# Attention and a routed mixture of experts on one core: small slot tiles in column groups, w2 loaded by turns, another start

## The chip, the cores and the metric

The kernel runs on one core of one Trainium2 chip. The metric is the device time of an execution in microseconds, lower being better. Three runs of the kernel before took 748.45, 749.07 and 749.04 us; the median is 749.04.

## What is computed

The reference, cut to what matters (B = 16 batches of S = 128 tokens, D = 256):

```python
# attention, 16 heads of 64: the latents are the normed x, the context is ctx
x_n = layer_norm(ctx, ln1_w, ln1_b)
lat = layer_norm(layernorm(x), ln2_w, ln2_b) * (1 + cond) + cond
q   = lat @ Wq.T
k, v = split(concat(x_n, lat) @ Wkv.T)
x   = x + softmax(q @ k.T / 8) @ v @ Wo.T
# experts: 8 routed, of which each token takes one, and a shared one; F = 704
h      = layernorm(x)
scores = h @ router                       # best expert, gate = sigmoid(best score)
routed = (silu(g*h @ w1[e]) * (g*h @ w3[e])) @ w2[e]
shared = (silu(h @ ws1) * (h @ ws3)) @ ws2
out    = x + shared + routed
```

All data are float32.

## The kernel before, in words

The order of the instructions on every engine is written out by hand. [...]

**Start.** `idle_ps` (L99 to L100) is a row of WARM = 9 matmuls on zeros. The first two batches' x and ctx and the constants `vec`, and the weights wk, wv, wq, wo, come over the SP and ScalarE queues (L281 to L294). `first_inputs(i)` (L387) makes the normed, transposed and modulated inputs `kvT` of batch i: statistics on VectorE (DVE), a reciprocal root by `newton` (L121, twelve DVE steps on 128x2 values), scaling (`normed`, L139), transposes on TensorE into a PSUM tile `fkvt` (L410), and modulation (L416 on DVE, L418 on ScalarE). Then come the projections `k_unit` (L440), `v_unit`, `q_unit`.

**Attention.** `step` (L788) handles half the heads of a batch: logits, maxima, exponents, normalising, turning through DRAM, and the weighted sum `weigh` (L556). Projections of the next batches, output projections (`finish`) and units of the shared expert are put between as `units`. `weigh` writes two heads into rows 0 to 63 and 64 to 127 of one PSUM tile, two matmuls of 64 columns.

PSUM has three pools: `ps_m` (three buffers, one bank each) for most products, `ps_s` (two buffers of two banks) for logits and the experts' up-projections, and `ps_o`.

**Routing.** `route` (L997) runs on DVE beside units of the shared expert. It finds each token's expert, sorts the experts by load into windows 0 to 7, and gives each token a slot. Window w has WINDOWS[w] slots: 320, 288, 288, 288 and four times 256. Slots are held in tiles: tiles 2w and 2w+1 have 128 rows; the rest of windows 0 to 3 (64, 32, 32, 32 rows, `REST`) lies in tiles 16 to 19, one for each window. So there are 20 tiles, four of them small. `slot_table` (L954) builds a table of token numbers and gates by 16 matmuls `slots` (L983) from `at_row` (L976).

**Experts.** `load_experts` (L920) loads w2 of all eight experts into `wds` ahead of the routing; `load_up` loads w1 and w3 of a window's expert into one of three buffers, at an address that SP reads from the routing. The rows of h are gathered by GpSimd (`gather`, L1188), multiplied by their gates and transposed: for window 0 on TensorE (`transpose_inputs`, L1207, tile `px`), for the others by DVE and a way through DRAM (`turn_inputs`, `fetch_inputs`). In the loop over windows (L1319), `up` (L1243) makes the hidden values `mid_w` in six parts f; after part 0 of window w come the down-projections of window w-1 (`down_window`, `out_rows` L1276): six matmuls `yr` for each tile (L1279), whose stationary operand is the tile's hidden values, 128, 64 or 32 columns wide, and whose moving operand is w2, 256 wide. Its address in `wds` comes from a register of TensorE's sequencer, read at L1320. DVE adds the gathered shared part, and GpSimd scatters the rows to the output. There are two buffers each of inputs and hidden values. `ending` closes with the last block of the shared expert.

The lines for the small tiles:

```python
def tiles_of(w):
    return [2 * w, 2 * w + 1] + ([2 * E + w] if REST[w] else [])
def rows_of(t):
    return P if t < 2 * E else REST[t - 2 * E]
```

Of the kernel before, what the change touches and what calls it, by code (L numbers as in the profile page):

```python
# [20 lines left out]
WARM = 9  # L21
# [6 lines left out]
def resampler_attn__then__top1_moe_kernel(  # L28
# [40 lines left out]
    NTILE = 2 * E + NREST  # L69
# [189 lines left out]
    with ExitStack() as at:  # L259
# [17 lines left out]
        wk = wts.tile([P, DC, INNER], F32, name="wk")  # L277
# [5 lines left out]
        nc.scalar.dma_start(out=vec, in_=vecs)  # L283
        nc.sync.dma_start(out=wk, in_=wkv_t[:, 0:INNER].rearrange("(c p) e -> p c e", p=P))
        nc.scalar.dma_start(out=tokens[0][:, 1, :], in_=lat_ctx[1])
        nc.sync.dma_start(out=xres[0][:, 1, :], in_=x[1])
        nc.scalar.dma_start(
            out=wv, in_=wkv_t[:, INNER : 2 * INNER].rearrange("(c p) e -> p c e", p=P)
        )
        nc.scalar.dma_start(out=wq, in_=wq_t.rearrange("(c p) e -> p c e", p=P))  # L290
        nc.sync.dma_start(out=wr, in_=router.rearrange("(c p) e -> p c e", p=P))
        nc.scalar.dma_start(out=wo, in_=wo_t.rearrange("(k p) d -> p k d", p=P))
        nc.sync.dma_start(out=h_rows[NT : NT + 1, :], in_=zero[0:1, :])
        nc.sync.dma_start(out=s_rows[NT : NT + 1, :], in_=zero[0:1, :])  # L294
# [92 lines left out]
        def first_inputs(i):  # L387
# [14 lines left out]
            for r in newton(small, v, 2, "j2"):  # L402
                pass
            z = work.tile([P, 2, D], F32, tag="z", name=f"fz_{i}", bufs=1)
            for k, t in enumerate(pair):
                normed(z[:, k, :], t, (mv[:, k, 0:1], r[:, k : k + 1]))
            for c in range(DC):
                pt = ps_m.tile([P, 2, S], F32, tag="mm", name=f"fkvt_{i}_{c}")
                for k in range(2):
                    nc.tensor.transpose(pt[:, k, :], z[:, k, ts(c, P)], ident)  # L410
                for k, (w, o) in enumerate(
                    ((vec[:, c, C_W1 : C_W1 + 1], vec[:, c, C_B1 : C_B1 + 1]),
                     (mod_w[:, c, i : i + 1], mod_b[:, c, i : i + 1]))
                ):
                    if c == 0:
                        nc.vector.tensor_scalar(kvTs[0][:, c, i, k, :], pt[:, k, :], w, o, ALU.mult, ALU.add)  # L416
                    else:
                        nc.scalar.activation(  # L418
                            kvTs[0][:, c, i, k, :], pt[:, k, :], AF.Identity, bias=o, scale=w
                        )  # L420
# [19 lines left out]
        def k_unit(b, j):  # L440
# [3 lines left out]
            for jj in range(2):  # L444
                for c in range(DC):
                    nc.tensor.matmul(  # L446
                        pk[:, jj, :],
                        lhsT=wk[:, c, ts(2 * j + jj, P)],
                        rhs=kvTs[b // 2][:, c, b % 2].rearrange("p t s -> p (t s)"),
                        start=(c == 0),  # L450
                        stop=(c == DC - 1),
                    )
# [335 lines left out]
        def step(u, units, side, loads=(), early=4, behind=(), exp_first=False):  # L788
# [15 lines left out]
            if u // 2 >= B - 2:  # L804

                nc.scalar.activation(spare[0:1, 1:2], spare[0:1, 0:1], AF.Exp)
# [38 lines left out]
        load_tokens(1)  # L845
        pieces, transpose = inputs(1)
# [6 lines left out]
        def second_inputs():  # L853
            transpose(range(DC))
            load_tokens(2)

        choose = []
        for g in range(NG):
# [9 lines left out]
            if g == 0:  # L868
                step(0, k1[:2] + [second_inputs] + k1[2:] + q[:2], [])
# [47 lines left out]
    wds = wexp.tile([P, E, NF, D], F32, name="wds")  # L917
    w13s = [wexp.tile([P, DC, 2 * F], F32, name=f"w13_{k}") for k in range(3)]

    def load_experts():  # L920
        for e in range(E):
            nc.sync.dma_start(
                out=wds[:, e, 0:FC, :],
                in_=w2[e, 0 : FC * P, :].rearrange("(c p) d -> p c d", p=P),
            )
            nc.sync.dma_start(out=wds[:, e, FC, :], in_=w2[e, F - P : F, :])
# [70 lines left out]
    def route():  # L997
# [98 lines left out]

        slot = mscratch.tile([P, B], F32, name="slot")
        nc.vector.scalar_tensor_tensor(slot, win, 2.0 * P, place, ALU.mult, ALU.add)
        shift = mscratch.tile([P, B], F32, name="shift")
        nc.vector.tensor_scalar(  # L1100
            shift, win, -float(P), float((2 * E - 2) * P), ALU.mult, ALU.add
        )
        nc.vector.scalar_tensor_tensor(shift, place, 2.0 * P, shift, ALU.is_ge, ALU.mult)
        nc.vector.tensor_tensor(slot, slot, shift, ALU.add)

        def beyond(n, w, length, name, pool):

            o = pool.tile([P, length], F32, name=name)
            for k in range(E):
                step = REST[k] - (REST[k + 1] if k + 1 < E else 0)  # L1110
                if step:
                    less = mscratch.tile([P, length], F32, tag="less", name=f"{name}{k}")
                    nc.vector.tensor_scalar(less, w, float(k + 1), float(step), ALU.is_lt, ALU.mult)
                    nc.vector.tensor_tensor(o, n, less, ALU.subtract)
                    n = o
            return o

        over = beyond(place, win, B, "over", mconst)
# [15 lines left out]
        for n, _ in enumerate(finding):  # L1134
            if n == 0:
# [15 lines left out]
                for w in range(3):  # L1151
                    load_up(w, w)
            if n == 1:

                load = beyond(total, window, E, "load", mconst)
# [9 lines left out]
        for t in tiles_of(0):  # L1165
            gather(t)
        for _ in range(4):
            yield
        for t in tiles_of(0):
            gate(t)  # L1170
        yield
        for i, t in enumerate(tiles_of(0)):
            transpose_inputs(t, inputs_t[0][:, :, ds(i * P, rows_of(t))], rows_of(t))
        for t in tiles_of(1):
            gather(t)


    xgs, ups = {}, {}
    inputs_t = [rwork.tile([P, DC, WMAX], F32, name=f"xT_{k}", bufs=1) for k in range(2)]
    x_blocks = tc.dram_tile([DC, WMAX // BL, BL, NB, BL], F32, name="x_blocks")  # L1180

    def tiles_of(w):
        return [2 * w, 2 * w + 1] + ([2 * E + w] if REST[w] else [])

    def rows_of(t):
        return P if t < 2 * E else REST[t - 2 * E]

    def gather(t, n=None):  # L1188
        n = n or rows_of(t)
        xg = rwork.tile([P, D], F32, tag="xg", name=f"xg_{t}")  # L1190
        nc.gpsimd.indirect_dma_start(
            out=xg[0:n, :],
            out_offset=None,
            in_=h_rows,
            in_offset=Offset(ap=routing["table"][0:n, t : t + 1], axis=0),
            bounds_check=NT,
            oob_is_err=False,
        )
        xgs[t] = xg

    def gate(t, n=None):
        n = n or rows_of(t)
        nc.vector.tensor_scalar(
            xgs[t][0:n, :], xgs[t][0:n, :], routing["gates"][0:n, t : t + 1], None, ALU.mult
        )

    def transpose_inputs(t, xT, n):  # L1207
        xg = xgs.pop(t)
        px = ps_m.tile([P, DC, n], F32, tag="mm", name=f"px_{t}")
        for c in range(DC):  # L1210
            nc.tensor.transpose(px[:, c, :], xg[0:n, ts(c, P)], ident[0:n, 0:n])
        nc.vector.tensor_copy(xT, px)

    def turn_inputs(w):

        for i, t in enumerate(tiles_of(w)):
            n = rows_of(t)
            gate(t)
            px = rwork.tile([P, DC, NB, BL], F32, tag="xp", name=f"xp_{t}")
            nc.vector.transpose(  # L1220
                px[0:n], xgs.pop(t)[0:n, :].rearrange("p (c k j) -> p c j k", c=DC, k=BL)
            )
            nc.sync.dma_start(
                out=x_blocks[:, ds(i * NB, n // BL)].rearrange("c i k j q -> (i k) c (j q)"),
                in_=px[0:n].rearrange("p c j q -> p c (j q)"),
            )

    def fetch_inputs(w):
        n = WINDOWS[w]
        for c in range(DC):  # L1230
            nc.sync.dma_start(
                out=inputs_t[w % 2][:, c, 0:n].rearrange("p (i q) -> p i q", q=BL),
                in_=x_blocks[c, 0 : n // BL].rearrange("i k j q -> (k j) i q"),
            )

    def load_up(k, w):
        e = nc.sync.value_load(routing["expert"][0:1, w : w + 1], min_val=0, max_val=E - 1)
# [4 lines left out]

    def up(w13, xT, n, mid, f, name):  # L1243

        ps = ps_s.tile([P, 2, 512], F32, tag="S", name=f"u_{name}_{f}")
# [18 lines left out]
    def stream_rows(t, n, table=None):  # L1264
        sg = mwork.tile([P, D], F32, tag="xr", name=f"sg_{t}", bufs=3)
        nc.gpsimd.indirect_dma_start(
            out=sg[0:n, :],
            out_offset=None,
            in_=s_rows,
            in_offset=Offset(ap=routing["table"][0:n, t : t + 1], axis=0),  # L1270
# [5 lines left out]
    def out_rows(t, n, e, mid, sg):  # L1276
        py = ps_m.tile([P, D], F32, tag="mm", name=f"yr_{t}")
        for f in range(NF):
            nc.tensor.matmul(  # L1279
                py[0:n, :],  # L1280
                lhsT=mid[:, f, 0:n],
                rhs=wds[:, ds(e, 1), f, :].rearrange("p e d -> p (e d)"),
                start=(f == 0),
                stop=(f == NF - 1),
            )
# [13 lines left out]
    load_experts()  # L1299
# [11 lines left out]
    mids = [hidden_t.tile([P, NF, WMAX], F32, name=f"mid_w{k}") for k in range(2)]  # L1311
# [3 lines left out]
    def down_window(w, sgs):  # L1315
        for i, (t, sg) in enumerate(zip(tiles_of(w), sgs)):
            out_rows(t, rows_of(t), ups[w], mids[w % 2][:, :, ds(i * P, rows_of(t))], sg)

    for w in range(E):  # L1319
        ups[w] = nc.tensor.value_load(  # L1320
# [157 lines left out]
```

## Time and profile before

| what | value |
|---|---|
| runs | 748.45, 749.07, 749.04 us |
| profiled execution, its time | 748.45 us |
| its span, first to last instruction | 746.6 us |
| granted TensorE clock, mean | 0.999 |
| first projection (pk, L446) starts | 9.32 us |
| last matmul ends | about 741.2 us |
| VectorE, ScalarE, GpSimd busy | 385.8, 259.1, 314.4 us |
| HBM read, written | 75.49 MB, 49.02 MB |

How it is read: "busy" is the time in which an engine had at least one of its instructions running; PE is TensorE's matmul stream and PEld its weight loads. A group's line gives the source line, engine, operation, out<-in, shape and the number of records, then busy time and the mean of one in ns; after a second bar stands the idle time just before. A line of the waits gives who waited for whom: us in total, times, longest. A line of the chain gives start, duration and what. Times are from the span's start. "SPq" and "ACTq" are queues that issue transfers.

### The profile page before, as it was taken

What the parts mean: (1) busy time and instruction counts of PE and PEld (TensorE: products, weight loads), DVE (VectorE), ACT (ScalarE), POOL (GpSimd) and SP (SyncE); (2) the same over time, 40 slices, a digit from 0 to 9 for tenths busy, and PEclk for the clock granted to TensorE, in tenths of its full rate; (3) what the DMA queues carried; (4) which work ended last, traced back from release to release, by engine and by line L of the source; (5) the groups of instructions that cost most, each with busy time, mean ns of one, the idle gap of its engine ahead of it and who ended that gap; (6) DMA issues with size and microseconds to landing.
All of it is one profiled execution on the core that took longest, in us unless ns stands there. A gap on an engine that the chain in (4) does not pass through costs nothing.

```text
span 746.6 us, 11560 instructions
## 1 busy us (share of the span) xinstructions
PE 736.0 (99%) x4096; PEld 572.5 (77%) x4096; DVE 385.8 (52%) x949; ACT 259.1 (35%) x787; POOL 314.4 (42%) x366
## 2 busy tenths in 40 slices
PE   8999999999999999999999999999999999999997
PEld 6857768777677677687686788688888877778886
DVE  5566558558647656665656437634643333333321
ACT  2444534444354354344444554611311011111111
POOL 1363554464355445534643654440104334444220
PEclk9999999999999999999999999999999999999999
DMA  8075735844953953864664634651991345645301
GB/s 297 17 250 195 204 128 179 235 165 154 270 170 127 264 200 129 218 223 143 193 197 137 203 124 165 208 183 56 306 322 55 83 110 154 173 138 162 97 27 46
DMA packets 140773, 125.20 MB, mean 168 GB/s; under 512 B 62484, under 2 KB 124631, under 8 KB 140708
## 3 DMA queue, kind: packets, MB, share of 16 engines
q1 hardware_dynamic: 134356, 108.49, 46.8%
q0 software_dynamic: 4336, 12.46, 5.4%
q10 hardware_dynamic: 2016, 3.43, 1.3%
q8 instruction: 35, 0.57, 0.3%
q14 instruction: 30, 0.25, 0.1%
HBM read 75.49 MB, written 49.02 MB: 167 GB/s over the span
## 4 chain that ended last, share of the span: by engine, by line
PE 93%; DVE 4%; ACT 2%; issue 0%; DMA 0%; ACTq 0%
PE pk L446 15%; PE pv L465 14%; PE u_w L1249 11%; PE S L498 8%; PE O L563 8%; PE p L162 8%; PE pw L579 7%; PE pq L431 7%; PE yr L1279 7%; PE ys L192 5%; ACT pe L517 1%; PE pr L634 1%; PE pr L162 1%; PE ys L245 1%; PE slots L983 0%
## 5 line engine op out<-in xcount | busy, mean ns | idle before, releaser
L530 POOL TENSOR_SCALAR pe<-pe,rs 128x256 f32<-128x256 f32 x256 | 232.5, 926 | 243.7 <-DVE rs L527 243.7
L517 ACT ACTIVATE pe<-S,nmx 128x256 f32<-128x256 f32 x256 | 118.7, 489 | 132.0 <-DVE nmx L510 132.0
L465 PE MATMUL pv<-wv,kvT 128*128 128x512 f32 x256 | 116.5, 599 | 0.2 <-ACT kT L454 0.2
L446 PE MATMUL pk<-kvT,wk 128*128 128x256 f32 x512 | 115.2, 383 | 1.3 <-ACT kT L454 0.7
L446 PEld LDWEIGHTS pk<-kvT,wk 128*128 128x128 f32 x512 | 95.8, 190 | 19.4 <-DVE px L539 2.0
L539 DVE STREAM_TRANSPOSE px<-pe 128x512 f32<-128x512 f32 x128 | 81.4, 682 | 32.0 <-POOL pe L530 32.0
L465 PEld LDWEIGHTS pv<-wv,kvT 128*128 128x128 f32 x256 | 47.2, 190 | 53.2 <-issue 50.6
L1249 PE MATMUL u_w<-xT,w 128*128 128x256 f32 (+2 forms) x352 | 85.6, 399 | 0.3
L1249 PEld LDWEIGHTS u_w<-xT,w 128*128 128x128 f32 x352 | 66.0, 190 | 18.8 <-DVE mid_w L1258 3.3
L510 DVE TENSOR_REDUCE nmx<-S 128x4 f32<-128x1024 f32 x64 | 75.1, 1213 | 9.7 <-PE S L498 9.5
L162 PE MATMUL p<-hT,ws 128*128 128x256 f32 x320 | 73.8, 382 | 0.2 <-DVE mid L178 0.2
L162 PEld LDWEIGHTS p<-hT,ws 128*128 128x128 f32 x320 | 59.9, 190 | 10.0 <-issue 1.3
L563 PEld LDWEIGHTS O<-pT,v 128*64 128x64 f32 x1024 | 55.2, 137 | 14.7 <-issue 12.9
L498 PE MATMUL S<-kT,qT 64*128 64x256 f32 x512 | 63.9, 389 | 0.0
L563 PE MATMUL O<-pT,v 128*64 128x128 f32 x1024 | 63.0, 276 | 0.0
L472 ACT COPY v<-pv 128x512 f32<-128x512 f32 x64 | 38.2, 599 | 63.1 <-PE pv L465 63.1
L527 DVE RECIPROCAL rs<-sums 128x4 f32<-128x4 f32 x64 | 11.4, 177 | 93.4 <-ACT pe L517 93.4
L579 PEld LDWEIGHTS pw<-wo,oT 128*128 128x128 f32 x256 | 48.6, 190 | 12.2 <-issue 3.1
L579 PE MATMUL pw<-wo,oT 128*128 128x256 f32 x256 | 57.9, 379 | 0.0
L431 PE MATMUL pq<-kvT,wq 128*128 128x256 f32 x256 | 57.7, 379 | 0.0
L1257 ACT ACTIVATE rsl_w<-u_w 128x256 f32<-128x256 f32 (+2 forms) x40 | 16.0, 400 | 118.8 <-PE u_w L1249 118.8
L517 ACT ACTIVATION_READ_ACCUMULATOR pe<-S,nmx 128x1 f32 x256 | 56.6, 221 | 0.0
(212 smaller groups left out, 748.5 us busy)
## 6 DMA issues: line engine op xcount, KB each, us to landing
p_blocks<-px SPq DMA_DIRECT2D x64, 512.0 KB, 3.2
pT<-p_blocks SPq DMA_DIRECT2D x64, 512.0 KB, 4.2
w<-in_w_dram SPq DMA_DIRECT2D x8, 704.0 KB, 6.3
wds<-in_w_dram SPq DMA_DIRECT2D x8, 640.0 KB, 8.3
w<-in_w_dram SPq DMA_DIRECT2D x8, 640.0 KB, 5.6
t_blocks<-tx SPq DMA_DIRECT2D x12, 256.0 KB, 2.4
kvT<-t_blocks SPq DMA_DIRECT2D x12, 256.0 KB, 6.2
h_rows<-h SPq DMA_DIRECT2D x8, 256.0 KB, 3.1
```

Of the source, the lines that this page charges most:

```text
L162: nc.tensor.matmul(ps, lhsT=shared["w13"][:, c, ds(col, P)], rhs=hT[:, c, ts(t, TB)], start=(c == 0), stop=(c == DC - 1),)
L431: nc.tensor.matmul(pq[:, jj], lhsT=wq[:, c, ts(2 * j + jj, P)], rhs=kvTs[g][:, c, :, 1, :], start=(c == 0), stop=(c == DC - 1),)
L446: nc.tensor.matmul(pk[:, jj, :], lhsT=wk[:, c, ts(2 * j + jj, P)], rhs=kvTs[b // 2][:, c, b % 2].rearrange("p t s -> p (t s)"), start=(c = ...
L465: nc.tensor.matmul(pv, lhsT=kvTs[b // 2][:, c, b % 2, t, :], rhs=wv[:, c, ts(n, 512)], start=(c == 0), stop=(c == DC - 1),)
L498: nc.tensor.matmul(pl[:, r, j, :], lhsT=qTs[b // 2][rows, k, b % 2, :], rhs=kTs[b][rows, k, :], start=True, stop=True,)
L510: nc.vector.tensor_reduce(nmx, pl, AX.X, ALU.max, negate=True)
L517: nc.scalar.activation(pes[u][:, h, :], pl[:, r, j, :], AF.Exp, bias=nmx[:, r, j : j + 1], accum_out=sums[u][:, h : h + 1],)
L530: nc.gpsimd.tensor_scalar(w, w, rs[:, i : i + 1], None, ALU.mult)
L539: nc.vector.transpose(px[:, :, t].rearrange("p j h q -> p h j q"), pes[u][:, ts(n, 4), ts(t, S)].rearrange("p h (j k) -> p h j k", k=BL),)
L563: nc.tensor.matmul(o[r * HD : (r + 1) * HD, j, :], lhsT=vs[b][:, t, ts(2 * (4 * half + j) + r, HD)], rhs=pTs[u][:, j // 2, :, t, 2 * (j % ...
L579: nc.tensor.matmul(pw, lhsT=outT[2 * b + k // 4][:, k % 4, :], rhs=wo[:, k, :], start=(k == 0), stop=(k == NP - 1))
L1249: nc.tensor.matmul(ps[:, k, 0:n], lhsT=w13[:, c, ds(col, P)], rhs=xT[:, c, 0:n], start=(c == 0), stop=(c == DC - 1),)
```

## The change

The small tiles: the rests of windows 0 to 2 (64 + 32 + 32 rows) share one tile of 128 rows, tile 16, and that of window 3 is tile 17 with 32 rows. There are 18 tiles. Both are gathered ahead of window 0, transposed on TensorE, and copied in blocks of 32 columns to the inputs of their windows. Their down-projections run once, in window 4: tile 16 as 24 matmuls of 32 columns each, which go in turn to PSUM rows 0, 32, 64 and 96 with the w2 of three experts; tile 17 as 6. To that end there are four buffers of inputs and five of hidden values.

w2 is loaded for a window's expert by `load_down` into one of five buffers, at an address that SP reads, five of them during the routing, three in windows 4 to 6. TensorE reads no register any more.

The slot arithmetic on DVE follows the new numbering (`steps`, `ahead`, `beyond`). The sixth part of `up` takes its PSUM from `ps_m`.

The start: wk is split into two halves; vec, wk, wv, wq go over SP in the order of their use, and router, wo and two rows of zeros follow after the next tokens (`later_loads`). The first batch's root is a ScalarE Sqrt (its table loaded at once by an activation on a spare value), a DVE reciprocal and one Newton step; its scaling goes by halves of 128 columns, its two transposes go to PSUM tiles of two pools, and DVE and ScalarE modulate one each. Step 0 loads the exponential's table ahead, and its transposes stand one by one between the key units. WARM is 6.

```diff
-WARM = 9
+WARM = 6
-    NTILE = 2 * E + NREST
+    NTILE = 2 * E - (-sum(REST) // P)
...
-        nc.scalar.dma_start(out=vec, in_=vecs)
-        nc.sync.dma_start(out=wk, in_=wkv_t[:, 0:INNER].rearrange("(c p) e -> p c e", p=P))
+        nc.sync.dma_start(out=vec, in_=vecs)
         nc.scalar.dma_start(out=tokens[0][:, 1, :], in_=lat_ctx[1])
+        nc.scalar.activation(spare[0:1, 1:2], spare[0:1, 0:1], AF.Sqrt)
+        def load_keys(k):
+            nc.sync.dma_start(
+                out=wks[k],
+                in_=wkv_t[:, ts(k, INNER // 2)].rearrange("(c p) e -> p c e", p=P),
+            )
+        load_keys(0)
         nc.sync.dma_start(out=xres[0][:, 1, :], in_=x[1])
+        load_keys(1)
...
+        def later_loads():
+            nc.sync.dma_start(out=wr, in_=router.rearrange("(c p) e -> p c e", p=P))
+            nc.sync.dma_start(out=wo, in_=wo_t.rearrange("(k p) d -> p k d", p=P))
+            nc.sync.dma_start(out=h_rows[NT : NT + 1, :], in_=zero[0:1, :])
+            nc.sync.dma_start(out=s_rows[NT : NT + 1, :], in_=zero[0:1, :])
...
-            for r in newton(small, v, 2, "j2"):
-                pass
+            if i == 0:
+                root = small.tile([P, 2], F32, name="froot")
+                nc.scalar.activation(root, v, AF.Sqrt)
+                half = small.tile([P, 2], F32, name="fhalf")
+                nc.vector.tensor_scalar(half, v, -0.5, None, ALU.mult)
+                y = small.tile([P, 2], F32, name="fy")
+                nc.vector.reciprocal(y, root)
+                a = small.tile([P, 2], F32, name="fa")
+                nc.vector.tensor_tensor(a, y, y, ALU.mult)
+                nc.vector.tensor_tensor(a, a, half, ALU.mult)
+                r = small.tile([P, 2], F32, name="fr")
+                nc.vector.scalar_tensor_tensor(r, a, 1.5, y, ALU.add, ALU.mult)
+            else:
+                for r in newton(small, v, 2, "j2"):
+                    pass
...
+                for k, t in enumerate(pair):
+                    normed(z[:, k, ts(c, P)], t[:, ts(c, P)], (mv[:, k, 0:1], r[:, k : k + 1]))
+            for c in range(DC):
+                pt = [
+                    ps_m.tile([P, S], F32, tag="mm", name=f"fkvt_{i}_{c}_0"),
+                    ps_s.tile([P, 2, 4 * S], F32, tag="S", name=f"fkvt_{i}_{c}_1")[:, 0, 0:S],
+                ]
...
-            if u // 2 >= B - 2:
+            if u == 0 or u // 2 >= B - 2:
                 nc.scalar.activation(spare[0:1, 1:2], spare[0:1, 0:1], AF.Exp)
...
-                step(0, k1[:2] + [second_inputs] + k1[2:] + q[:2], [])
+                turns = [lambda c=c: second_inputs(c) for c in range(DC)]
+                step(0, k1[:1] + turns[:1] + k1[1:2] + turns[1:] + k1[2:] + q[:2], [])
...
-    wds = wexp.tile([P, E, NF, D], F32, name="wds")
+    w2s = [wexp.tile([P, NF, D], F32, name=f"w2_{k}") for k in range(5)]
...
+        def steps(w, length, name, marks):
+            o = None
+            for k, n, op in marks:
+                for _ in range(n // BL):
+                    a = mscratch.tile([P, length], F32, name=f"{name}{k}_{op.name}", tag=name, bufs=2)
+                    if o is None:
+                        nc.vector.tensor_scalar(a, w, float(k), None, op)
+                    else:
+                        nc.vector.scalar_tensor_tensor(a, w, float(k), o, op, ALU.add)
+                    o = a
+            return o
...
-                for w in range(3):
-                    load_up(w, w)
+                load_up(0, 0)
+                load_down(0, 0)
+                load_up(1, 1)
+                load_down(1, 1)
+                load_up(2, 2)
+                for w in range(2, 5):
+                    load_down(w, w)
...
+        first = [2 * E, 0, 1] + list(range(2 * E + 1, NTILE))
...
+        for w, at, to in rests[t - 2 * E]:
+            nc.vector.tensor_copy(inputs_t[w][:, :, ds(to, BL)], px[:, :, ds(at, BL)])
...
+    def load_down(k, w):
+        e = expert_of(w)
+        a2 = w2[ds(e, 1)]
+        nc.sync.dma_start(
+            out=w2s[k][:, 0:FC, :],
+            in_=a2[:, 0 : FC * P, :].rearrange("e (c p) d -> p (e c) d", p=P),
+        )
+        nc.sync.dma_start(
+            out=w2s[k][:, FC, :], in_=a2[:, F - P : F, :].rearrange("e p d -> p (e d)")
+        )
...
         for f in range(NF):
-            nc.tensor.matmul(
-                py[0:n, :],
-                lhsT=mid[:, f, 0:n],
-                rhs=wds[:, ds(e, 1), f, :].rearrange("p e d -> p (e d)"),
-                start=(f == 0),
-                stop=(f == NF - 1),
-            )
+            for rows, mid, wd in parts:
+                nc.tensor.matmul(
+                    py[rows, :], lhsT=mid[:, f, :], rhs=wd[:, f, :], start=(f == 0), stop=(f == NF - 1)
+                )
...
+    def down_rests(sgs):
+        for k, parts in enumerate(rests):
+            out_rows(
+                2 * E + k,
+                [(slice(at, at + BL), mids[w][:, :, ds(to, BL)], w2s[w]) for w, at, to in parts],
+                sgs[k],
+            )
...
+                if w == NREST:
+                    down_rests(rest_sgs)
...
+                if NREST <= w < E - 1:
+                    load_down((w + 1) % 5, w + 1)
```

## The prediction

> **What bounds the kernel now.** I read the page first, then the list of waits, then the chain over the first 40 us, then the matmul groups by shape, then TensorE's timeline over the experts. Page, part 1 and the PE row of part 2:
>
> ```profile
> PE 736.0 (99%) x4096; PEld 572.5 (77%) x4096; DVE 385.8 (52%) x949; ACT 259.1 (35%) x787; POOL 314.4 (42%) x366
> PE   8999999999999999999999999999999999999997
> ```
>
> TensorE works from the first slice to the last. All its waits on another engine, in full:
>
> ```profile
> PE idle_ps L100 <- DVE idle L97: 1.3, 1, 1.3
> PE slots L983 <- DVE at_row L976: 0.8, 1, 0.8
> PE pk L446 <- ACT kT L454: 0.7, 1, 0.7
> PE pk L446 <- DVE kvT L416: 0.7, 1, 0.7
> PE fkvt L410 <- DVE fz L140: 0.6, 1, 0.6
> PE px L1211 <- DVE mid L178: 0.5, 1, 0.5
> PE pv L465 <- ACT kT L454: 0.2, 1, 0.2
> PE p L162 <- DVE mid L178: 0.2, 1, 0.2
> ```
>
> They add to 5.0 us; the rest of the idle time is the 5.4 us after the last matmul (741.2 to 746.6), which the change does not touch. So from the first projection at 9.32 us on, time comes only from fewer TensorE microseconds, from starting earlier, or from those few waits. Busy DVE, DMA and register work elsewhere is worth nothing by itself. The start, from the chain:
>
> ```profile
> 5.09 0.17 DVE j2h L124
> ...
> 7.13 0.17 DVE j2y L135
> 7.30 0.03 issue
> 7.33 0.42 DVE fz L140
> 7.75 0.14 issue
> 7.89 0.58 PE fkvt L410 x2
> 8.46 0.03 issue
> 8.49 0.74 DVE kvT L416 x2
> 9.23 0.09 issue
> 9.32 7.33 PE pk L446 x32
> ```
>
> Until 7.3 us the chain is a DVE Newton root, not a weight transfer; TensorE's busy time before that is the nine warm-up matmuls on zeros.
>
> **Packed small tiles.** By shape (count is records; an fp32 matmul leaves two, one per pass):
>
> ```profile
> L563 PE MATMUL O<-pT,v 128*64 128x128 f32 x1024 | 63.0, 276 | 0.0
> L1279 PE MATMUL yr<-wds,mid_w 128*128 x192 | 42.7, 379 | 0.0
> L1279 PE MATMUL yr<-wds,mid_w 128*32 x36 | 8.3, 381 | 0.0
> L1279 PE MATMUL yr<-wds,mid_w 128*64 x12 | 2.8, 383 | 0.0
> ```
>
> A 32-column down-projection matmul costs what a 128-column one does (8.3/36 = 0.23 us a pass, against 42.7/192 = 0.22). In TensorE's timeline the down-projections of windows 0 to 3 run 603.32 to 611.32, 622.39 to 630.37, 641.43 to 649.41 and 660.26 to 668.25: 31.95 us; without a small tile they take 5.18 us (678.18 to 683.36). So the four small tiles cost 31.95 - 4 x 5.18 = 11.2 us, on the bound. After: one tile of 24 matmuls in four column groups, and one of 6 in one group. The 6 cost 12 passes x 0.216 = 2.6 us. The 24 take, with all four groups running at once, 12 x 0.216 = 2.6 us; one by one 48 x 0.216 = 10.4 us. No row shows four groups. The nearest is O, two groups of 64 columns: single starts come in pairs 7 ns apart every 109 ns, for 128 moving columns, exactly the 109 ns between single px transposes of the same length. Two groups are thus fully concurrent, and every 16-matmul block holds 16 clean pairs, so groups are really interleaved and not chained pass on pass. One matmul and weight load leave per 54.5 ns there; four groups at 256 columns ask for one per 216/4 = 54 ns, so dispatch is shown to keep up, and each weight load is half as wide. Only four moving streams at once are unseen. Entering the 32-column form costs 0.1 us (309 ns to the first record instead of 216). I take 2.7 + 2.6 = 5.3 us: **-5.9 us**; bounds -5.9 (four at once) and +1.9 (one at a time, loads hidden).
>
> Against this stands the Trainium skill, TensorE: Matmul & The Clock Gate, Part 3 (Packing small matmuls), The mechanism: a weight load runs under a matmul in flight only when its row group differs. Column groups share the row group. By that rule each of 48 passes would show its load (106 to 110 ns in the 32-wide rows) as well: 48 x (0.216 + 0.110) = 15.6 us, and the part would be +7.0 us. The O row speaks against it: same row group, loads of 137 ns, and still 54.5 ns per record. I go by the row and keep the rule as the losing rival.
>
> **Start.** The 12 DVE steps of Newton take 7.33 - 5.07 = 2.26 us. They become a ScalarE root (0.3 us, estimate: an accumulator read of one column is 0.2 and a semaphore hop under 0.1), a reciprocal (0.18) and three DVE steps at 0.2 each: 1.1 us, half hidden under the root: -1.15. From the root to the first projection (1.99 us now) the four half-width scalings take about 0.95, the second transpose and its hop 0.15, and the two modulations run side by side on DVE and ScalarE (0.41 and 0.46) instead of 0.74 in series, into separate PSUM tiles: about 1.5, -0.5. The ScalarE table load (1.28 us at 7.74), which now delays the second input half to 9.85 and so the second projection by 0.24 us, moves to about 1.7 us, where ScalarE is idle: -0.24. Sum **-1.9 us**, bounds -1.2 (root hop 0.6, halves save nothing) and -2.3. With Sqrt loaded first, the changed program holds a second table load ahead of the first exponential; ScalarE stands idle for 1.74 us there (26.84 to 28.57), so it is covered; uncovered it would cost ScalarE 1.3 us, of which TensorE sees at most the 0.7 below.
>
> Weights: in the first 9.3 us queues move 244 GB/s on average and the key weights land at about 8.4. In one queue, ahead of the first half of wk stand 148 KB (x, vec), beside it 256 KB of ctx on the other: at the 300 GB/s of this stage its 512 KB are there at about 6, needed at 7.7. Halves of wk, wv, wq follow at about 8, 11 and 13.5, needed at 11, 15.5 and 17. vec (small rows, now trickling between 4 KB packets until 7.3) no longer does, so the modulation constants on GpSimd are ready in time. What is queued behind on SP: the next tokens (needed only by DVE work with 7 us to spare), router, wo and the zero rows (first used tens of us later). Price: nothing; if the first half were late, up to 1.5 us, all of the start's gain.
>
> Three warm-up matmuls less leave TensorE idle from about 5.9 to 6.6 us. The switch from 427 to 216 ns per pass came at 5.1 us, so six still reach it. Cost 0. If the array fell back to the slow rate for as long as its first slow stretch (1.3 to 5.1 us), it would cost half of that, +1.9.
>
> **First step.** Splitting the second pair's transposes puts each between two key units, so a PSUM buffer that waited for ScalarE's copy is asked for one unit later: the 0.7 us wait of pk on kT goes. **-0.7**, bounds 0 and -0.7.
>
> **Routing.** DVE works without pause from 533.99 to 545.4 and TensorE already waits 0.8 us for at_row. The tile numbering gets 17 small steps for 14 (+0.63 at 0.21 each), the load count one less (-0.2), the three wide steps are 10% narrower (-0.1): **+0.35**, bounds 0 and +0.8.
>
> **Turning the rest tiles.** One more pair of transposes (+0.22). The packed tile is copied out in four pieces of about 0.2 us instead of one of 0.31, and the next hidden unit needs that PSUM buffer: +0.45. **+0.65**, bounds +0.2 and +1.0.
>
> **w2 by turns.** 5.8 MB ahead of the routing become 3.6 MB behind the expert numbers, which come at about 541.7 us. SP issues 19 loads at some 0.57 us; with w1 and w3 7.9 MB at the 306 to 322 GB/s of slices 29 and 30 are in by about 567, and the first is used at 584, w2 at 603. Later turns have a 15 us window each, and on SP the fetch of the next inputs stands ahead of them. Register loads vanish from TensorE's sequencer, where the timeline shows no gap for them. 0.
>
> **Sum.** -5.9 - 1.9 - 0.7 + 0.35 + 0.65 = -7.5 us. The profiled execution took 748.45 us (span 746.6); 740.95. The median of the three runs is 0.6 above it, at 749.04: 741.6.
>
> **Rivals.** (a) Two groups at a time (four streams exceed what feeds the array): the packed tile takes 5.2, total 744.2. For: only two are seen. Against: dispatch and loads have room. 12%. (b) The start gains nothing, since the one queue or the cold clock gives it back: 743.5. Against: the transfer estimate has 1.5 us to spare. 8%. (c) The packing doesn't do what it says, groups one by one with loads hidden: 749.4, no change. 5%. (d) Slower: groups one by one with their loads exposed, at the packed tile in window 4, 15.7 us: -7.5 + 13.0 = +5.5, 754.5. It decides once that tile takes longer than 11.7 us (2.7 + 7.5 + 1.5). 9%. (e) The forecast, 740.0 to 743.2: 66%.
>
> The range 740.0 to 745.5 holds (e), (a) and (b), less their tails. A measurement tells 0.2% (1.5 us) from no change; (e), (a), (b) are faster, 0.86; (c) same, 0.05; (d) slower, 0.09.
>
> **What would show it.** Packed records starting four together every 216 ns, 2.7 us in all; pairs mean (a), singles (c), singles 326 ns apart (d). First projection at about 7.4 to 7.9 us, no wait on a weight; no wait of pk on kT near 31 us; slots waiting about 1.2 us; the hidden unit after px waiting about 0.4. A new TensorE wait on a w2 or wk transfer would make the forecast wrong.

## The result, and the profile after

The changed kernel takes 739.04 us (median of five runs, 738.8 to 741.31; one of the five lies 2.3 above the median, see the warm-ups below) beside 749.04 us (748.45 to 749.07): a ratio of 0.9874, interval 0.986 to 0.9887. The profiled execution took 739.16 us, its span is 737.4 us. The gain is 10.0 us by the medians and 9.3 between the two profiled executions; the forecast had 7.4 and 7.5. The last matmul starts 9.5 us earlier (740.80 before, 731.29 after), so nearly all the gain lies ahead of it.

The page of the changed kernel, part 1:

```profile
span 737.4 us, 11471 instructions
PE 727.1 (99%) x4104; PEld 569.9 (77%) x4104; DVE 383.6 (52%) x946; ACT 261.1 (35%) x791; POOL 309.5 (42%) x363
```

TensorE is still full, with 8.9 us less busy time in 8 records more. The waits in its row of matmuls, on other engines and transfers, from the list of waits:

```profile
PE idle_ps L100 <- DVE idle L97: 1.3, 1, 1.3
PE slots L1013 <- DVE at_row L1006: 1.1, 1, 1.1
PE fkvt L440 <- DVE fz L140: 0.6, 1, 0.6
PE pk L481 <- DMA wk<-in_wkv_t_dram: 0.5, 1, 0.5
PE px L1258 <- DVE mid L178: 0.5, 1, 0.5
PE pv L500 <- ACT kT L489: 0.2, 1, 0.2
PE p L162 <- DVE xT L1265: 0.2, 1, 0.2
PE p L162 <- DVE mid L178: 0.2, 1, 0.2
```

Against the list of before: the wait of pk on kT in step 0 is gone and slots wait 0.3 us longer, both as forecast. A wait on a half of wk is new. The list adds to 4.6 us, hardly less than the 5.0 of before, so it does not tell where 10 us came from. The matmul groups by shape tell more than half of it:

```profile
L1349 PE MATMUL yr<-w,mid_w 128*32 128x256 f32 x60 | 5.4, 381 | 0.0
```

The narrow down-projections, 8.3 + 2.8 us in 48 records before, are 5.4 us in 60. In TensorE's records the 48 passes of the packed tile start in fours, 6 to 7 ns apart, and the fours stand 216 ns apart. Only the step from the first four to the second is longer, 241 ns. All four column groups run at once.

The rest was found by laying starts of the two traces beside each other. The stretch from the last down-projection of one window to the first of the next (start to start, us) has no small tile in it, and yet it shrank at nearly every window:

| kernel | w0-1 | w1-2 | w2-3 | w3-4 | w4-5 | w5-6 | w6-7 |
|---|---|---|---|---|---|---|---|
| before | 11.37 | 11.37 | 11.16 | 10.25 | 10.05 | 10.05 | 9.71 |
| changed | 10.89 | 10.88 | 10.67 | 9.91 | 9.71 | 9.71 | 9.71 |
| e1, changed, sixth part in `ps_s` | 11.18 | 11.18 | 10.96 | 10.25 | 10.05 | 10.05 | 9.71 |
| e2, before, sixth part in `ps_m` | 11.08 | 11.08 | 10.87 | 9.91 | 9.71 | 9.71 | 9.71 |

The forecast had nothing at all here. The last two rows belong to the experiments. (A stretch named w0-1 lies behind the down-projections of window 0.)

### The profile page after: what moved, and what is told of

It reads as the page before. It is cut to its first block, busy times and chain, and to the rows that moved or that the text cites. A ratio compares the mean times of both kernels' runs of the same rounds, so it can differ in the third digit from the quotient of the medians.

```text
span 737.4 us, 11471 instructions
## 1 busy us (share of the span) xinstructions
PE 727.1 (99%) x4104; PEld 569.9 (77%) x4104; DVE 383.6 (52%) x946; ACT 261.1 (35%) x791; POOL 309.5 (42%) x363
## 4 chain that ended last, share of the span: by engine, by line
PE 94%; DVE 3%; ACT 1%; DMA 1%; issue 0%; SPq 0%; ACTq 0%
PE pk L481 15%; PE pv L500 14%; PE u_w L1316 10%; PE S L533 8%; PE O L598 8%; PE p L162 8%; PE pw L614 7%; PE pq L466 7%; PE yr L1349 6%; PE ys L192 5%; PE ur_w L1316 1%; PE pr L669 1%; DMA wk<-in_wkv_t_dram 1%; PE pr L162 1%; PE ys L245 1%; ACT pe L552 0%
## 5 line engine op out<-in xcount | busy, mean ns | idle before, releaser
L500 PEld LDWEIGHTS pv<-wv,kvT 128*128 128x128 f32 x256 | 47.2, 190 | 53.2 <-issue 50.6
L1316 PE MATMUL u_w<-xT,w 128*128 128x256 f32 (+2 forms) x320 | 77.1, 396 | 0.0
L1316 PEld LDWEIGHTS u_w<-xT,w 128*128 128x128 f32 x320 | 60.7, 190 | 13.7 <-issue 0.4
```

The lines of the kernel that those rows point to most:

```text
L500: nc.tensor.matmul(pv, lhsT=kvTs[b // 2][:, c, b % 2, t, :], rhs=wv[:, c, ts(n, 512)], start=(c == 0), stop=(c == DC - 1),)
L1316: nc.tensor.matmul(ps[:, k, 0:n], lhsT=w13[:, c, ds(col, P)], rhs=xT[:, c, 0:n], start=(c == 0), stop=(c == DC - 1),)
```

## The experiments

The kernel before ran beside every group of runs: its median was 748.42 us beside e1 to e4, 748.78 beside e5 to e9, and 748.54 beside e10 to e13. The changed kernel itself ran beside the second group only (e9); elsewhere its 739.0 us stands for it, and the kernel before differs by 0.6 us between its measurements; so a difference well under 1 us counts there only where the traces show it too.

### What shortened the window boundaries: e1, e2, e3

In the trace of before, the timeline around such a boundary shows a stall that TensorE's own row does not. In the kernel before, from the last parts of window 0 to part 0 of window 1 (start, duration, engine, line, what; in brackets the idle time ahead of it and what ended it):

```profile
599.79 2.48 PE L1249 MATMUL u_w<-xT,w 128*128 128x320 f32 x8
...
600.73 0.49 DVE L1258 TENSOR_TENSOR mid_w<-u_w,rsl_w 128x320 f32<-128x320 f32 x1 [1.66 <-ACT rsl_w L1257]
601.27 0.78 PEld L1249 LDWEIGHTS u_w<-xT,w 128*128 128x128 f32 x4 [0.48 <-DVE mid_w L1258]
```

The weight load at 601.27 waited for the VectorE product that ended at 601.22. The PE row is one bar of eight records without a gap. The starts of its records do have one: 406 ns where 269 is the rule, then 347 where 242 is, 0.24 us lost. Theory one: that product reads the PSUM buffer of part f = 4. Parts 4 and 5 hold both buffers of `ps_s`, so part 0 of the next window waits until VectorE has released the first. The change moved part 5, the sixth, to `ps_m`, a line that the forecast gave no cost. Theory two: the stall came from TensorE's register, read once in a window and used in each down-projection.

**e1**, the changed kernel with that line undone:

```diff
-        if f < FC:
-            ps = ps_s.tile([P, 2, 512], F32, tag="S", name=f"u_{name}_{f}")
-        else:
-            ps = ps_m.tile([P, 1, 512], F32, tag="mm", name=f"ur_{name}")
+        ps = ps_s.tile([P, 2, 512], F32, tag="S", name=f"u_{name}_{f}")
```

> The changed kernel with one thing undone: the sixth part of up takes its PSUM from ps_s again, as before the change. The stretches from the last down-projection of one window to the first of the next are 0.24 to 0.40 us shorter in the changed kernel in seven of eight places, 2.4 us in all, which the forecast did not have. Theory one (PSUM): part 0 of the next window had to wait for the PSUM buffer that DVE releases after part 4 of this one, since parts 4 and 5 hold both buffers of ps_s. Then this kernel gives back 2.0 to 2.4 us and takes about 741.2 us, and gaps of 400 ns between matmul starts come back at the boundaries. Theory two (register): the gap came from the register that TensorE read once in a window and in each down-projection. Then this kernel takes the 739.0 us of the changed one.

Measured: 741.06 us (740.98 to 741.17), ratio 0.9899 [0.9884, 0.9914].

**e2**, the kernel before with the same line put in, nothing else:

> The kernel before with one part of the change alone: the sixth part of up takes its PSUM from ps_m. The PSUM theory expects 2.0 to 2.4 us less, about 746.8 us, a ratio of 0.997. The register theory expects no change, 749.0 us, since the register reads stay.

Measured: 746.25 us (746.09 to 747.06) beside 748.42, ratio 0.9972 [0.9961, 0.9983].

**e3**, the kernel before without the register:

```diff
-        ups[w] = nc.tensor.value_load(
-            routing["expert"][0:1, w : w + 1], min_val=0, max_val=E - 1
-        )
+        ups[w] = w
...
-                rhs=wds[:, ds(e, 1), f, :].rearrange("p e d -> p (e d)"),
+                rhs=wds[:, e, f, :],
```

> The kernel before with TensorE's register taken away: the down-projections of window w take w2 of expert w at a fixed address, whatever expert the routing named (so the routed rows are those of the wrong expert; shapes and number of operations are unchanged). The register theory expects 2.0 to 2.4 us less, 746.8 us. The PSUM theory expects no change, 749.0 us within 0.3, and the 400 ns gaps at the window boundaries stay.

Measured: 748.41 us beside 748.42, ratio 0.9999 [0.999, 1.0007].

Done alone the edit gains 2.2 us, beside the kernel before on the same chip. Undone it costs 2.0, against the changed kernel's 739.04 us, which was measured apart from it. Without the register nothing moves. In the table above, e1 and the changed kernel differ by 0.29, 0.30, 0.29, 0.34, 0.34, 0.34 and 0.00 us; before and e2 by 0.29, 0.29, 0.29, 0.34, 0.34, 0.34 and 0.00. The stretch ahead of the first down-projection adds 0.25 in both pairs: 2.15 us. The PSUM theory stands, the register theory falls. The list of waits had the stall all along, in the rows of the weight loads (PEld). The kernel before:

```profile
PEld u_w L1249 <- DVE mid_w L1258: 3.3, 7, 0.5
```

The same row of e1 (changed, part 5 back in `ps_s`):

```profile
PEld u_w L1313 <- DVE mid_w L1322: 2.9, 6, 0.5
```

The kernel before waits seven times, once for each boundary; e1's list has six of them. In e3, where the register is gone, the row is that of before to the digit. The lists of e2 and of the changed kernel have no such row. Its 3.3 us is more than the 2.15 it cost, since part of each wait of a load lies under a matmul still running: at the boundary above the load waited 0.48 us, and the matmul starts lost 0.24.

### What the order of the packed matmuls is worth: e4

```diff
-        for f in range(NF):
-            for rows, mid, wd in parts:
+        for rows, mid, wd in parts:
+            for f in range(NF):
```

> The changed kernel with the 24 matmuls of the packed tile issued group by group (six for rows 0 to 31, then six for rows 32 to 63, and so on) instead of in turn. Theory: the four groups run at once only when they follow one another in the stream, so the tile goes from 12 steps of 216 ns to 48: from 2.6 to 10.4 us, with loads hidden, and the kernel takes 739.0 + 7.8 = 746.8 us. If the loads of 32 columns are not hidden within a group (the rule on row groups), 48 passes of about 326 ns: 15.6 us and 752 us. If the order in the stream does not matter, 739.0.

Measured: 743.32 us, ratio 0.9929 [0.9916, 0.9943]; 4.3 us more than the changed kernel, and none of the three numbers expected. The narrow group in e4:

```profile
L1349 PE MATMUL yr<-w,mid_w 128*32 128x256 f32 x60 | 9.8, 381 | 0.0
```

That is 4.4 us more than the 5.4 above. In its records, single starts stand 216 ns apart, but at each change of group four pairs follow (5 ns apart, then 31, 31, 31). The records do not name their column group, but two chains of 216 ns lie in each other there, and the first pass of the new one is drawn 404 ns long, as the first passes of the groups in the changed kernel are (403). The old group's chain runs on for three more passes after the new one has begun. So the first four passes of the new group run beside the last four of the old. Four changes (the last one to tile 17) hide four passes each, so 60 passes take 44 steps of 216 ns, 9.5 us, and 0.1 to enter the form. So the order matters, and TensorE reaches about four passes ahead into a free column group. Neither the expected 7.8 us nor the rule on row groups, which the prediction cites, holds: within a group the passes stand 216 ns apart and not 326, so the loads stay hidden.

### What the start and the first step are worth: e9, e5, e6, e8

These four ran on one chip, beside the kernel before at 748.78 us. **e9** is the changed kernel itself:

> The changed kernel itself, so that the next three are compared on one chip with it: 739.0 us, 0.9874 of the kernel before.

Measured: 739.00 us (738.45 to 739.07), ratio 0.987 [0.9854, 0.9886]. In its profile the first projection starts at 7.63 instead of 8.07, and no wait on wk is left. The chain of the changed kernel, first profile, ran through the transfer:

```profile
1.76 6.17 DMA wk<-in_wkv_t_dram
7.93 0.14 issue
8.07 7.16 PE pk L481 x32
```

In e9 it runs through the inputs:

```profile
7.12 0.47 ACT kvT L449
7.59 0.04 issue
7.63 4.44 PE pk L481 x19
```

The same program, and the start differs by 0.4 us: the half of wk stands on the edge.

**e5**, the transposes of step 0 together again:

```diff
-step(0, k1[:1] + turns[:1] + k1[1:2] + turns[1:] + k1[2:] + q[:2], [])
+step(0, k1[:2] + turns + k1[2:] + q[:2], [])
```

> The changed kernel with the splitting of the second pair's transposes in step 0 undone. The forecast's term, read from the list of waits: the 0.7 us wait of pk on kT comes back, +0.7 us. A second reading, from the shift of the first logits of half-batch 1 between the two traces (-1.42 before them, -2.37 after): +0.95 us, because a stall counts as busy until the modelled end of the matmul before it. If the step gained nothing and the shift had another cause: 0.

Measured: 739.76 us (739.62 to 739.82), +0.76. From the first logits of half-batch 0 to those of half-batch 1 it takes 14.31 us, as before (14.31); the changed kernel takes 13.36, so 0.95 in the trace. The wait is back in its list:

```profile
PE pk L481 <- ACT kT L489: 0.7, 1, 0.7
```

The step is worth 0.8 to 0.95 us; the times cannot tell the two readings apart, but the trace has the second.

**e6**, the first half of wk on two queues:

```diff
         nc.sync.dma_start(out=vec, in_=vecs)
+        nc.scalar.dma_start(out=wks[0][:, 1, :], in_=wkv_t[P : 2 * P, 0 : INNER // 2])
+        nc.sync.dma_start(out=wks[0][:, 0, :], in_=wkv_t[0:P, 0 : INNER // 2])
         nc.scalar.dma_start(out=tokens[0][:, 1, :], in_=lat_ctx[1])
...
-        load_keys(0)
```

> The changed kernel with the first half of wk on two queues, 256 KB each, behind the first ctx on ScalarE's queue and behind vec on SP's, ahead of the second ctx and x. The first projection waits 0.5 us for a half of wk that lands at 7.9 us; its inputs are ready at 7.6. If the one queue is what made it late, the half is there by 7.5 and the first projection starts 0.3 to 0.5 us earlier: 738.6 us. If the 16 engines move these rows of 2 KB no faster from two queues, or the second inputs come too late now: 739.0 or up to 0.3 more.

Measured: 738.95 us (738.89 to 738.98), ratio 0.9869 [0.9852, 0.9885]: no gain over e9. Its first projection starts at 7.76, 0.04 us after its inputs. Its chain ran through the warm-ups, the last of which ended at 6.74. Nothing was left to win where wk was in time already, so whether two queues help an execution in which wk is late is not shown.

**e8**, the root by twelve VectorE steps again:

```diff
-            if i == 0:
+            if i < 0:
                 root = small.tile([P, 2], F32, name="froot")
```

> The changed kernel with the first batch's root by twelve VectorE steps again (the ScalarE root and the one Newton step undone; transfers, halves and table loads as in the changed kernel). The forecast put the root at 1.15 us. If the first projection were bound by the inputs alone, it starts 1.1 us later: 740.1. If the key weights bind it now (they land at 7.9, the inputs are ready at 7.6), 0.4 of it is hidden: +0.7, 739.7.

Measured: 740.86 us, four runs at 740.14, 740.23, 741.5 and 741.89; ratio 0.9891 [0.9875, 0.9908]. The profiled one took 741.89. The root takes 2.26 us there (5.12 to 7.38) against 1.02 in e9 (4.98 to 6.00), so it is worth 1.24. But the first projection starts at 9.01 and its first passes take 427 ns. TensorE's granted clock (seventh value, PEclk) by stretches of 2 us in e8:

```profile
6.00:8.00 2.00, 0.45 (x3) 0.13 (x1) 1.72 (x10) 0.00 (x0) 0.00 (x0) 1.00 0.99 335
8.00:10.00 2.00, 1.89 (x7) 1.19 (x8) 1.97 (x8) 0.91 (x2) 0.00 (x0) 0.81 1.04 422
10.00:12.00 2.00, 2.00 (x7) 1.55 (x6) 1.69 (x13) 0.00 (x0) 0.00 (x0) 0.50 1.01 410
```

TensorE had stood idle from 6.35 to 7.90. The clock is half from 9.22 to 12.64: eight passes of the projection take 427 ns each instead of 216, 1.7 us more in all. The four runs fall into two pairs, 1.1 to 1.2 us over e9 and 2.5 to 2.9. The first is what the root alone costs; the traced execution, of the second pair, has the root and the clock. The expectation missed this; what it said of the wk transfer can't be read from these runs.

### What the warm-ups are worth: e10, e13

**e10** sets WARM = 9, **e13** WARM = 4, in the changed kernel.

> The changed kernel with nine warm-up matmuls again instead of six. The forecast put the three taken away at 0. Since then two traces were seen in which TensorE's change from 427 to 216 ns per pass came at 4.3 and at 6.1 us after the same start, so nine end between about 6.5 and 7.6 us, while the inputs of the first transposes are ready at about 6.5. First theory: they hold the start up, and this kernel is 0.2 to 1.0 us slower than the changed one: 739.2 to 740.0, with the spread of its runs under 1 us. Second theory: the warm-ups cost nothing in either number: 739.0. If the idle time after six warm-ups costs clock in most executions, this kernel is faster by up to 1.

> The changed kernel with four warm-up matmuls instead of six. They end at about 4.8 us, at the slow rate, and TensorE stands idle until 6.5. Theory: the switch to 216 ns asks for TensorE to be busy for some 3 to 5 us and an idle stretch of 1.5 us or more undoes it (in the run with the root on VectorE, idle from 6.2 to 7.9, eight passes of the first projection took 427 ns, 1.7 us). Then the first projection has 8 to 16 passes of 427 ns here, and the kernel takes 740.7 to 742.4 us. Rival: the array keeps its rate, or changes at a fixed time whatever it did: 739.0.

e10 measured 739.51 us (738.87, 739.07, 739.96, 740.35), ratio 0.9877 [0.9862, 0.9892]; e13 740.45 us (740.2 to 741.96), 0.9898 [0.9883, 0.9914]. TensorE's timeline of e13:

```profile
6.47 1.00 PE L440 MATMUL fkvt<-ident,fz 128*128 128x128 f32 x4 [1.81 <-DVE fz L140]
7.80 3.53 PE L481 MATMUL pk<-kvT,wk 128*128 128x256 f32 x8 [0.32 <-DVE kvT L441]
```

After 1.8 us without work, the first projection again has seven passes of about 427 ns, which cost 1.5 us over passes of 216; e13's median is 1.4 over the changed kernel's. In e10's profile (740.35 us) the change to 216 ns came only at 7.4 us; the nine warm-ups ran to 8.3, and the first transposes, whose inputs are there at about 6.5 in the changed kernel, waited. So four are too few and nine cost 0 to 1.3 us, by the moment at which the clock changes. The second holds for the profiled execution; e10's median lies within its own spread of the changed kernel's, and its other three runs have no trace.

### A better version: e11, e12

If four groups run at once, the 32 rows of tile 17, alone in 12 steps of 216 ns, can be spread over several groups. Both kernels load the same 32 columns into several groups, each of which takes a part of the columns of w2 (`ways` is 2 in e11, 4 in e12, for tile 17 alone):

```diff
+        half = D // ways
         for f in range(NF):
             for rows, mid, wd in parts:
+                for g in range(ways):
                     nc.tensor.matmul(
-                        py[rows, :], lhsT=mid[:, f, :], rhs=wd[:, f, :], start=(f == 0), stop=(f == NF - 1)
+                        py[slice(rows.start + g * BL, rows.stop + g * BL), 0:half],
+                        lhsT=mid[:, f, :], rhs=wd[:, f, ts(g, half)],
+                        start=(f == 0), stop=(f == NF - 1),
                     )
+        if ways > 1:
+            side = mwork.tile([P, WMAX], F32, tag="sl", name=f"side_{t}")[:, 0:D]
+            for g in range(ways):
+                nc.scalar.activation(side[0:BL, ts(g, half)], py[ts(g, BL), 0:half], AF.Identity)
+            py = side
```

> The changed kernel with tile 17 (32 rows) spread over two column groups: the same 32 stationary columns are loaded into both, each takes 128 of the 256 columns of w2, ScalarE brings the two pieces side by side, VectorE adds as before. Theory: the groups run at once, so the tile takes 12 steps of 109 ns instead of 216, 1.3 us less: 737.7 us. If a step of a second group costs its full length after all: 739.0. If the new ScalarE copies hold up the hidden units behind them: 739.0 to 739.6.

> The same with four column groups, each with 64 columns of w2. If four short matmuls run at once and leave fast enough: 12 steps of 55 ns, 1.9 us less than the changed kernel: 737.1 us. If TensorE sends off a matmul with its load no faster than one in about 30 ns (the spacing seen where two groups overlapped), a step takes 120 ns and nothing is won over two groups: 737.6 to 737.9. If one in 54.5 ns is the limit (the spacing of O), a step takes 218: no gain, 739.0.

e11 measured 737.54 us (737.47 to 737.76), ratio 0.9854 [0.9839, 0.9869]; e12 737.07 us (736.7 to 737.32), 0.9848 [0.9835, 0.9862]. The group of tile 17 in e12, 24 instructions of 64 columns:

```profile
L1352 PE MATMUL yr<-w,mid_w 128*32 128x64 f32 x48 | 0.9, 219 | 0.0
```

Four start within 20 ns, and the next four 56 ns after the first: 14 ns per pass with its load. Neither of the two limits in the expectation (30 and 54.5 ns) exists at this length. The traces carry the gain: from the first down-projection of window 3 to the last of the rest tiles it takes 10.26 us in the changed kernel, 9.10 in e11 and 8.52 in e12, and the stretch behind it 9.91, 9.80 and 9.75. That is 1.3 and 1.9 us less. e12 is the fastest kernel of the study.

## Why the forecast was right in direction and too small

| step of the forecast | forecast, us | trace, us | by an edit of its own |
|---|---|---|---|
| packed small tiles | -5.9 | -5.56 in the blocks, -0.57 behind them | order alone 4.3 (e4) |
| start | -1.9 | -1.42 (first profile), -1.76 (e9) | root alone 1.2 (e8) |
| first step | -0.7 | -0.95 | 0.76 (e5) |
| routing | +0.35 | +0.54 | |
| turning the rest tiles | +0.65 | +0.59 | |
| sixth part of `up` to `ps_m` | not costed | -2.15 | 2.0 (e1), 2.2 (e2) |
| w2 by turns, register | 0 | 0 | 0.0 for the register (e3) |
| sum | -7.5 | -9.5 with the first profile's start | |

The sum of the trace's column, -9.5, meets the 9.5 us by which the last matmul moved; behind it the end takes 5.7 us instead of 5.5.

**The step that failed** is the one that opens the forecast: "All its waits on another engine, in full". The list given was that of TensorE's matmul row. The rows of its weight loads were left out, and with them seven waits on VectorE at the window boundaries, 2.15 us. The page of before, which the forecast says was read first, shows them too, as the last entry of this row:

```profile
L1249 PEld LDWEIGHTS u_w<-xT,w 128*128 128x128 f32 x352 | 66.0, 190 | 18.8 <-DVE mid_w L1258 3.3
```

With those waits unseen, the edit of `up` looked like bookkeeping and got no term in the sum. From it followed the wrong rule that time comes only from "fewer TensorE microseconds, from starting earlier, or from those few waits". With 2.15 us more in its sum the forecast would have been 739.45, beside the 739.04 measured. That this is so near is in part luck, since the other errors run both ways: the packed tiles +0.3 us in the blocks and -0.6 behind them, the start +0.5, the first step -0.25, routing +0.2, turning -0.1, the end +0.2. By the medians the miss is 2.6 us, by the profiled executions 1.8: the one before lay 0.6 us under its median, the one after 0.1 above.

**Packed tiles.** The blocks of windows 0 to 3 took 7.91, 7.89, 7.89 and 7.89 us before and 5.18, 5.18, 5.18 and 10.48 after: 5.56 less. The tile and its neighbour cost 5.3 as the sum had it. The forecast counted 0.1 us for entering the narrow form, but not the return to wide matmuls behind it: 0.19 us at each of three boundaries (e2 against the changed kernel in the table), which vanish too. The O row was the right guide, and the rule on row groups would have given 754.5. The plain rows of before spoke against it as well: the 128-column `yr` passes start 216 ns apart while their loads, in the same row group, take 190.

**Start.** The root brought 1.24 instead of 1.15, the way from root to projection 0.4 instead of 0.5, and the second projection gained 0.1 (e9) on the first instead of 0.24. The term that cost most in the first profile is the transfer: "at the 300 GB/s of this stage its 512 KB are there at about 6, needed at 7.7". In the changed kernel's first profile that half landed at 7.93 and cost 0.4; in e11, whose start is the same, it waited 0.4 as well, and in e9, e4 and e12 it was in time. The forecast named a wait on wk as the sign that would make it wrong. It came in two of the seven kept traces of this start, for less than the 1.5 us allowed.

**First step.** The wait list gave 0.7 and the trace 0.95. Idle time is counted from the modelled end of the last matmul, 272 or 379 ns after its start, where the next may start after 109 or 216: a stall's first 0.16 us counts as busy. The same hides most of the boundary stalls.

**Routing and turning.** Routing is off by 0.2. `slots` starts 0.31 us later, as the +0.35 had it, and waits 1.1 us (1.2 forecast). The other 0.23 comes ahead of it, where a weight load of `p` now waits 0.37 us for VectorE's `mid`: again a row that the forecast did not read. Turning is off by less than 0.1: px and the unit behind it wait 0.5 and 0.2, and up to the first up-projection TensorE is 0.59 us later.

**Warm-ups** at 0 held in the traced executions, by a small margin that the forecast did not see: 0.6 us (changed kernel) and 0.85 (e11) without work kept the clock, 1.55 (e8) and 1.8 (e13) lost it. Of the execution that took 741.31 us no trace is kept. Its mean granted clock was 0.997, as in the traced executions of e8 and e13 that lost the clock, against 0.998 to 0.999 in the other four; so it may have lost it too, which is not shown.

That w2 by turns costs nothing was not tried by itself. TensorE has no wait on w2 in the changed kernel.

## What to carry to other kernels

Read an engine's waits in all of its rows: on TensorE, a wait for a PSUM buffer ends at the weight load, and the matmul row hides it, because each matmul is drawn longer than the spacing at which the next could start. Not every wait of a load costs time, though: before the change the loads of `pv` wait 206 times, 50.6 us in all, and yet nearly all of its passes start 429 ns apart in a row. So lay start times of a repeated stretch beside the spacing that its passes should have; a gap of 406 ns where 269 is the rule is a wait, whatever the busy share says. An edit that only moves a tile to another pool is an edit of the waits, and needs a price like any other.

## What the runs showed that was not expected

- Four column groups of 32 run fully at once: four passes of 256 columns together take 216 ns, four of 64 together 56 ns. A narrow tile left alone can be spread over the groups by splitting the moving columns (e12: 1.9 us).
- TensorE does not keep strictly to the order of the stream across column groups: the first four passes of a new group ran beside the last four of the old one (e4, read from the spacing of the records).
- The time at which warm-up passes go from 427 to 216 ns varies between executions of nearly equal starts: 4.3 us (e4), 5.1 (changed), 6.0 (e1), 7.4 (e10). From then on the granted clock changed in steps of 3.41 us: in e8 it was full from 5.81, half from 9.22 and full from 12.64, in e13 from 4.14, 7.56 and 10.97. So in e8 the clock fell 1.3 us after TensorE had work again. In the 3.41 us ahead of the fall its matmul row was busy for 1.75 us (e8) and 1.53 (e13); in such stretches of the changed kernel (2.33) and of e3 (2.10) the clock stayed full. Where an idle time falls among these steps should then decide whether it costs anything, which would explain the two pairs of e8, but only one of its executions is traced. The Trainium skill, TensorE: Matmul & The Clock Gate, Part 1 (The HAM clock gate), states a window of about 3.4 us that runs freely, whatever the kernel does: one busy window brings the full clock, one idle window takes it. The steps of 3.41 us and the 3.1 us over which the first change was spread agree with the window; that it must be idle does not, for a window about half busy was enough in these two runs.
